# A graph-attention layer: head-key bursts in pairs over two sets of PSUM pairs, row flags through DRAM, 64-output matmuls first in the attention sum

## The chip, the cores and the metric

The kernel runs on one core of one Trainium2 chip, in one launch. The time is device microseconds of one execution of the whole program; the figure given for a kernel is the median over its runs. A profile is one more execution, recorded by the hardware profiler. The engines are PE (TensorE, the matrix unit, which loads 128-row weights and streams columns of up to 512 against them), DVE (VectorE), ACT (ScalarE), POOL (GpSimd) and SP (which here only starts transfers). PE writes to PSUM, eight banks of 128 partitions by 512 floats; the other engines read the results there and "evacuate" them to SBUF, the on-chip memory that everything else lives in. DMA queues move data between SBUF and DRAM. Each engine works off its own queue in order; between engines there are semaphores only, set by the framework wherever one instruction reads what another has written or reuses a buffer that another has read.

## The reference, cut to what matters

A graph-attention layer over x (16 x 512 x 512, float32), with 16 heads of 32, and only the first 20 nodes of each batch as neighbours, in two directions d (the mask and its transpose):

```python
row_zero = v.sum(-1) == 0
q_exp = where(row_zero[..., None], 0.0, q[:, None, :])
self_feat = concat([v, q_exp], -1) @ W_self.T + b_self
output = self_feat
for d in range(2):
    A = (adj if d == 0 else adj.swapaxes(1, 2))[:, :, :20, :]
    cond, vb = A.sum(-1), A @ w_bias + b_bias
    kv = self_feat[:, :20]
    qh = heads(self_feat @ Wq[d].T + bq[d]);  kh = heads(kv @ Wk[d].T + bk[d])
    aff = where(cond > 0, qh . kh / sqrt(32), NEG) + vb
    output += heads_out(softmax(aff) @ kv, Wout[d]) + bout[d]
result = v + relu(output)
```

Three things of it matter here. The term of q enters a row only where the row's sum isn't zero, so each batch needs 512 *row flags*, 0 or 1, on all 128 partitions. The scores need no q projection per row: Wq is multiplied into the keys once, which gives 512 "head keys" per head, neighbour and direction, and the scores are then one product of `self_feat` with them. And the output projection is multiplied into the neighbours' features once (the "values").

## The kernel before, in words

**Stages.** The kernel has a setup, and then a loop over the 16 batches. The setup loads the weights, makes the neighbours' features `kvT` (512 x 320: 16 batches of 20), and from them all keys, values and biases; the loop makes `self_feat` of a batch, its scores in four tiles of 128 rows, the softmax and the weighted sum of the values (`attend`). The first products of batch 0 are made at the end of the setup.

**Bursts of head keys.** `key_rows` (the kind "r" below; PSUM tile `ps_k`, L588) makes 128 rows of the keys per call, as differences to neighbour 0, so 19 columns per batch; there are 8 calls, 2 directions by 4 groups of four heads. A unit of head-key work is one group of 128 output features, one group of four heads, one direction and one batch. There are 512 units, taken 25 or 26 at a time: 20 *bursts*, each of one to three *runs* of consecutive batches (mostly two). In `keys(runs)` a run is four matmuls (L676), one for each head of its group, on 32 rows and 128 outputs, with 19 columns per batch, up to 304. The four heads go to the four banks of two pairs of PSUM banks; a pair is one tile of the pool `ps_s`, which has two of them, so one burst fills the pool and the next has to wait until both are read. For each run ACT (L691) evacuates the first pair, for two heads, and DVE (L693) the second. Both write the tile `st`; when a group's last run is there, POOL copies batch 0's part to `g0` (L697) and SP stores the rest to `g1_d` and `g_d` in DRAM.

**Blocks between the bursts.** Between two bursts PE gets a *block* of other work, during which ACT and DVE empty the pairs. The blocks use single banks of the pool `ps_acc`, of which there are four, by `bank(name)`. Their kinds are

- "m", `bias_terms` (DVE alone), "b", `biases`: DVE adds `bq` to `bqw` (L610), ACT makes four pieces of `bqbd` (L612), POOL adds two small ones;
- "c", `bias_scores`: four small matmuls into `ps_c` (L624), then ACT's copy into the stage `c` (L629), POOL's addition (L633) and four small DMAs on POOL's queue to `cq_d` (L635), which `load_cq` later reads back;
- "v" and "w", `values`: one step is eight matmuls of 512 columns into `ps_v` (L649), and four steps make a result, which DVE copies (L655) and POOL's queue stores to `vw_d` (L659);
- "n", `row_flags` of batch 0 or 1: one matmul of 512 columns with a 128x128 matrix of ones (`ps_nz`, L213), which sums the row sums over the partitions onto all 128 of them, and DVE's test into `nzs[b]`;
- "p", `block_product`: one of the seven products of batch 0 (banks of 256 columns, L283), then a step of `partial` or `joined` on DVE.

The first matmul of `row_flags(b)` needs `row_sums(b)`: three additions on POOL (L207, L209) into a tile `rx` of the tag "xn". That tag has two buffers; `rx0`, the stage `c` and `rx1` take turns in them.

**Order.** Nothing is planned by the framework; everything is in the order in which it is written (`manual_schedule`), per engine. The loop over the bursts writes, after each burst, its block by a list of kinds, and after that the work of other engines for batch 0, by the burst's number: `mask_mul`, `mask_count`, `mask_sum` and `mask_spread` (POOL's product with the label weights, L314; DVE's count and POOL's test, L323; DVE's sum, L328; ACT's copies), `clear_first` (POOL's queue, zeros to `bd_d`, L148), `row_sums(1)`, `blocks(0)` (only makes a list of copies in DRAM), `load_cq(0)`, `new_self(0)` and `x_sum`, six `spill`s (each a copy of that list on POOL's queue) and `full_add`.

**attend.** Each batch's values are laid out so that the sum over 40 neighbours is done in pieces of 32 rows: four pieces with 32 outputs and then two with 64, each on four row groups, all added in the same four banks (L435). The first kind starts the addition, the second ends it.

The old order of blocks, one word for each burst from the fifth to the last, and the list of `attend`:

```python
plan = "mmvv bvv vvc vvc vvn vvw vvw vw wn p p p p p p p".split()
for first, runs in ((True, ((0, 1, 0), (3, 1, 2), (4, 1, 2), (7, 1, 4))), (False, ((1, 2, 1), (5, 2, 3)))):
```

Of the kernel before, what the change touches and what calls it, by code (L numbers as in the profile page):

```python
# [18 lines left out]
def gat_kernel(  # L19
# [20 lines left out]
    nc = tc.nc  # L40
    B, F, N = xT.shape
# [23 lines left out]

    def bank(name, at=None):

        tag = {} if at is None else {"bufs": 1}
        return acc["pool"].tile([P, 512], F32, tag="acc" if at is None else f"acc{at}", name=name, **tag)

    ctx.enter_context(tc.manual_schedule())

# [111 lines left out]
    def spill(n, queue=nc.sync):  # L184

        for _ in range(n):
            queue.dma_start(*copies.pop(0))
# [21 lines left out]
            nc.gpsimd.tensor_add(t, t, xs[b][:, k])  # L209

    def row_flags(b):
        ps = bank(f"ps_nz{b}")
        nc.tensor.matmul(ps[:, :N], ones, rss[b], start=True, stop=True)  # L213
        nzs[b] = load.tile([P, N], F32, tag="nz", name=f"nz{b}")
        nc.vector.tensor_scalar(nzs[b], ps[:, :N], 0.0, None, ALU.not_equal)


    def weight_sums():
# [100 lines left out]
    def mask_count(b, h):  # L319
        a = adjs[b, h]  # L320
        cond = msk.tile([P, 2 * S], F32, tag="cond", name=f"cond{b}_{h}")
        nc.vector.tensor_reduce(cond, a.rearrange("p t (m l) -> p (t m) l", l=L), AX.X, ALU.add)
        nc.gpsimd.tensor_scalar(prods[b, h][:, :, L], cond, 0.0, NEG, ALU.is_le, ALU.mult)  # L323
# [102 lines left out]
    def attend(b, banks, tiles=slice(0, NT), start=True, stop=True):  # L426


        wt = wts[b][:, tiles].rearrange("p t (g w) -> p (t g) w", g=HL)
        vd = vds[b].rearrange("p e i g -> p (e i g)")  # L430
        for first, runs in ((True, ((0, 1, 0), (3, 1, 2), (4, 1, 2), (7, 1, 4))), (False, ((1, 2, 1), (5, 2, 3)))):
            for at, n, j in runs:
                for a in range(HL):
                    r = bass.ts(a, R)
                    nc.tensor.matmul(  # L435
                        banks[a][bass.ds(at // 2 * DH, n * DH)].rearrange("p (t n) -> p t n", n=32),
                        vd[r, bass.ds(at * DH, n * DH)], wt[r, :, bass.ts(j, 32)],
                        start=start and first, stop=stop and not first,
                    )
# [15 lines left out]
        outs.clear()  # L455


    with tc.tile_pool(name="setup", bufs=1) as sp, tc.tile_pool(name="ps_acc", bufs=4, space=PSUM) as acc["pool"]:
        wq_sb = sp.tile([P, 2, C, F], F32, name="wq_sb")
        wo_sb = sp.tile([P, 2, C, F], F32, name="wo_sb")  # L460
        khD = sp.tile([P, 2 * C, B * ND], F32, name="khD")
# [15 lines left out]
        with tc.tile_pool(name="setup_k", bufs=1) as sk:  # L477
# [11 lines left out]
            for k in range(C):  # L489
# [1 line left out]
                    out=sel, in_=sel, pattern=[[-1, B]], compare_op=ALU.not_equal, fill=1.0,  # L491
                    base=-k * DH, channel_multiplier=1,
                )
            warm = bank("ps_warm")
            for _ in range(7):
                nc.tensor.matmul(warm[:, :P], ones, ones, start=True, stop=True)

# [85 lines left out]
            def key_rows(d, jc):  # L583

                ps = bank(f"ps_k{d}{jc}")
                for k in range(C):
                    for a in range(HL):
                        nc.tensor.matmul(  # L588
                            ps[bass.ts(a, R), :BM], wk_sb[d][:, k, bass.ds(jc * P + a * R, R)], kvT[:, k],
                            start=(k == 0), stop=(k == C - 1),  # L590
                        )
# [26 lines left out]
        with tc.tile_pool(name="setup_g", bufs=4) as sg:  # L618
# [82 lines left out]
            def block_product(n):  # L701
# [7 lines left out]
                f(*args)  # L709


            steps = {
                "b": [(biases, ())],
                "c": [(bias_scores, (d,)) for d in range(2)],
                "m": [(bias_terms, (d, c)) for c in range(C) for d in range(2)],
                "n": [(row_flags, (b,)) for b in range(2)],
                "p": [(block_product, (n,)) for n in (1, 2, 6, 7, 5, 4, 3)],
                "v": [(values, (t, (d,), k)) for t in range(2) for d in range(2) for k in range(C)],
                "w": [(values, (2, (0, 1), k)) for k in range(C)],
            }  # L720
# [13 lines left out]
            rest = [(d, hg) for hg in range(C) for d in range(2)]  # L734
            first = None
            for n, runs in enumerate(bursts):
                for i in range(len(rest)):
                    if i < (4 if n == 0 else 1) or any(fc == 0 and (d, hg) == rest[0] for fc, hg, d, _, _ in runs):
                        key_rows(*rest.pop(0))
                if n == 4:  # L740
                    values(*steps["v"].pop(0)[1])
                keys(runs)
                if rest:
                    for kind in "mm" if n else ():
                        f, args = steps[kind].pop(0)
                        f(*args)
                    continue
                first = n if first is None else first
                for kind in plan[n - first] if n - first < len(plan) else ():
                    f, args = steps[kind].pop(0)  # L750
                    f(*args)
                if n == 7:
                    mask_mul(0, 0)
                if n == 8:
                    mask_count(0, 0)
                if n == 10:
                    mask_sum(0, 0)
                    load_cq(0)
                if n == 7:
                    clear_first()  # L760
                if n == 9:
                    row_sums(1)
                    copies = blocks(0)
                if n > 13:
                    spill(1, nc.gpsimd)
                if n == 11:
                    new_self(0)
                    for i in range(1, 5):
                        x_sum(0, i)
                if 10 < n < 15:  # L770
                    mask_spread(0, 0, (n - 11,))
                if n == 14:
                    mask_mul(0, 1)
                if n == 15:
                    mask_count(0, 1)
                if n == 17:
                    full_add(0, 0)
# [308 lines left out]
```

## Time and profile before

| | us |
|---|---|
| median of 3 runs | 582.9 (582.06 to 583.93) |
| the profiled execution's own time | 582.57 |
| its span in the profile | 580.7 |
| PE busy | 574.0 (99%) |
| DVE, POOL, ACT busy | 489.8, 404.2, 395.8 |
| mean granted clock of PE | 0.999 |
| first burst to first block product | 26.10 to 72.30 |
| first block product to the loop | 72.30 to 91.33 |
| the loop and the end | 91.33 to 580.70 |

All times within the execution are microseconds from the start of the span. A row of the chain of work that ended last gives the start, the length, the engine and the group of instructions. A row of the groups of instructions gives the busy time, the engine, the line, the operation, out<-in with shapes, the count and, in brackets, the idle time of that engine just before and what ended it. PEld is PE's loading of weights, which overlaps the matmuls. "Busy" for PE is from the first to the last of a sequence of pipelined matmuls, with their ends modelled.

### The profile page before, as it was taken

The page shows a single profiled execution, that of the slowest core. Times are in us where ns is not written, and L with a number is a line of the kernel's source. Part 1 is how long each engine was busy: PE and PEld are TensorE (multiplying, and loading weights), DVE is VectorE, ACT ScalarE, POOL GpSimd, SP SyncE. Part 2 cuts the span into 40 slices and gives each one's busy share as a digit, 9 for nine tenths or more (in the row PEclk, how much of TensorE's full clock was granted, in tenths as well). Part 3 has the DMA queues.
Part 4 walks back from the last instruction along what each step waited for, and adds up shares of the span by engine and source line. Part 5 has one row for each costly group of instructions (what it writes and reads, how often), then busy time and mean ns, then how long its engine had stood idle before and what let it go on. Part 6 is the DMA issues. An engine that isn't in the chain of part 4 may idle for free.

```text
span 580.7 us, 30994 instructions
## 1 busy us (share of the span) xinstructions
PE 574.0 (99%) x13496; PEld 431.6 (74%) x13496; DVE 489.8 (84%) x786; ACT 395.8 (68%) x1170; POOL 404.2 (70%) x383
## 2 busy tenths in 40 slices
PE   8999999999999999999999999999999999999996
PEld 6444458878878787878778787887887878787873
DVE  0475676979898989898999999898989898989896
ACT  1334454587877777778786868687887877777671
POOL 2626976748687776858585867786868677685875
PEclk9999999999999999999999999999999999999999
DMA  8998997857675767777576767566657666674404
GB/s 290 387 399 300 332 362 274 231 144 222 202 239 177 215 200 198 218 181 229 171 215 166 219 166 219 166 205 181 202 162 223 197 191 182 196 205 109 148 19 146
DMA packets 98787, 123.26 MB, mean 212 GB/s; under 512 B 18876, under 2 KB 66968, under 8 KB 96604
## 3 DMA queue, kind: packets, MB, share of 16 engines
q1 hardware_dynamic: 96124, 117.80, 65.5%
q0 software_dynamic: 1392, 2.43, 1.8%
q8 instruction: 106, 1.74, 1.2%
q10 hardware_dynamic: 1136, 1.06, 0.5%
q14 instruction: 29, 0.24, 0.1%
HBM read 82.30 MB, written 40.24 MB: 211 GB/s over the span
## 4 chain that ended last, share of the span: by engine, by line
PE 94%; DVE 3%; DMA 1%; issue 0%; POOL 0%; SPq 0%; ACT 0%; DVEq 0%; POOLq 0%; ACTq 0%
PE ps_s L365 45%; PE ps_a L283 19%; PE ps_c L283 9%; PE ps_o L435 5%; PE ps_d L283 5%; PE ps_v L649 3%; PE ps_k L588 3%; DMA ws_q<-in_wsT 1%; PE ps_kv L537 1%; DVE o L444 0%; PE ps_nz L213 0%; DVE o L1023 0%; DVE wt L424 0%; DVE ps_s L383 0%; DVE sm L415 0%
## 5 line engine op out<-in xcount | busy, mean ns | idle before, releaser
L365 PEld LDWEIGHTS ps_s<-g,sf 128*32 128x32 f32 x8192 | 263.0, 110 | 21.5 <-issue 13.9
L365 PE MATMUL ps_s<-g,sf 128*32 128x152 f32 x8192 | 278.1, 293 | 0.3 <-issue 0.2
L337 ACT COPY both<-add 32x80 f32<-32x80 f32 x512 | 130.9, 256 | 60.3 <-DVE add L328 54.4
L417 POOL TENSOR_TENSOR s<-s,sm 128x640 f32<-128x640 f32 x63 | 80.2, 1274 | 95.5 <-DVE sm L416 73.4
L344 POOL TENSOR_TENSOR full<-cq,both 128x640 f32<-128x640 f32 x64 | 100.3, 1567 | 27.1 <-issue 21.2
L317 ACT ACTIVATE prod<-adj,wb_sb 128x80 f32<-128x80 int32 x330 | 112.4, 432 | 0.0
L392 ACT ACTIVATE s<-s 128x640 f32<-128x640 f32 x63 | 46.5, 738 | 56.5 <-DVE s L387 56.1
L449 POOL TENSOR_TENSOR o<-o,x 128x512 f32<-128x512 f32 x60 | 76.6, 1299 | 0.0
L379 DVE TENSOR_TENSOR full<-ps_s,full 128x608 f32<-128x608 f32 x63 | 48.7, 773 | 22.5 <-PE ps_s L365 19.2
L283 PE MATMUL ps_a<-t,ws_s 128*32 128x246 f32 x1024 | 60.0, 371 | 0.0
L415 DVE TENSOR_REDUCE sm<-s 128x32 f32<-128x640 f32 x63 | 50.8, 807 | 10.6 <-ACT s L392 10.4
L383 DVE TENSOR_REDUCE ps_s<-full 128x32 f32<-128x640 f32 x63 | 52.2, 828 | 2.2
L424 DVE STREAM_TRANSPOSE wt<-s 128x640 f32<-128x640 f32 x63 | 52.8, 838 | 0.6 <-POOL s L417 0.6
L387 DVE TENSOR_TENSOR s<-full,ps_s 128x640 f32<-128x640 f32 x63 | 51.5, 818 | 1.1
L289 DVE SCALAR_TENSOR_TENSOR sf<-nz,qw,ps_a 128x246 f32<-128x246 f32 x128 | 51.6, 443 | 0.3
L283 PEld LDWEIGHTS ps_a<-t,ws_s 128*32 128x32 f32 x1024 | 33.9, 110 | 17.5 <-issue 0.9
L328 DVE TENSOR_REDUCE add<-prod 128x80 f32<-128x960 f32 x32 | 36.8, 1149 | 6.8 <-ACT prod L317 4.0
L446 ACT ACTIVATE o<-o,bo 128x512 f32<-128x512 f32 x60 | 38.2, 709 | 0.6 <-DVE o L444 0.6
L248 POOL TENSOR_TENSOR t<-x 128x492 f32<-128x492 f32 x32 | 36.7, 1148 | 1.6 <-DMA g_d<-st 1.5
L248 POOL TENSOR_TENSOR t<-x,t 128x492 f32<-128x492 f32 x32 | 36.7, 1148 | 1.3
L435 PE MATMUL ps_o<-wt,vd 32*32 32x512 f32 (+5 forms) x816 | 37.6, 578 | 0.0
L444 DVE TENSOR_TENSOR o<-ps_o,sf 128x512 f32<-128x512 f32 x60 | 36.7, 668 | 0.0
(225 smaller groups left out, 712.6 us busy)
## 6 DMA issues: line engine op xcount, KB each, us to landing
g<-g_d SPq DMA_DIRECT2D x60, 304.0 KB
g_d<-st SPq DMA_DIRECT2D x16, 1064.0 KB
out_T<-o SPq DMA_DIRECT2D x60, 256.0 KB
xn<-in_xn SPq DMA_DIRECT2D x56, 256.0 KB
x<-in_xT SPq DMA_DIRECT2D x56, 256.0 KB
adj<-in_adj SPq DMA_DIRECT2D x60, 220.0 KB
nz<-nz_d SPq DMA_DIRECT2D x14, 256.0 KB
wk<-in_wkT SPq DMA_DIRECT2D x2, 1024.0 KB
```

What stands on the lines that cost most here:

```text
L248: done["xsum"] = nc.gpsimd.tensor_sub(t, one, two)
L283: nc.tensor.matmul(to, lhs, x[:, k], start=start, stop=stop, skip_group_check=n != 2)
L289: done["partial"] = nc.vector.scalar_tensor_tensor(to[:, i], nzs[b][:, half(l)], qw[:, 2 * f + i, b : b + 1], parts[b, "a"][i][:, :HN], AL ...
L317: nc.scalar.activation(p[:, :, l], a[:, :, l], AF.Identity, scale=wb_sb[:, l : l + 1])
L337: done["spread"] = nc.scalar.copy(adds[b, h][bass.ts(a, R), :, g], add[r].rearrange("p (t m) -> p t m", t=2))
L344: done["full"] = nc.gpsimd.tensor_add(f, cqs[b].unsqueeze(1).to_broadcast(shape), adds[b, nt // 2][:, nt % 2].unsqueeze(2).to_broadcast(sh ...
L365: nc.tensor.matmul(to, sfs[b][:, k, bass.ds(nt * P + (2 * g + j) * R, R)], of, start=(onto is None and k == 0 and (whole or j == 0)), stop ...
L383: nc.vector.tensor_reduce(mx, f, AX.X, ALU.max)
L417: done["normal"] = nc.gpsimd.tensor_mul(s, s, sm.unsqueeze(3).to_broadcast(full))
L424: nc.vector.transpose(wts[b][:, nt], s.rearrange("p a h m -> p (a h m)"))
L435: nc.tensor.matmul(banks[a][bass.ds(at // 2 * DH, n * DH)].rearrange("p (t n) -> p t n", n=32), vd[r, bass.ds(at * DH, n * DH)], wt[r, :, ...
L449: nc.gpsimd.tensor_add(o[:, c], o[:, c], xs[b][:, c])
```

## The change

Four things are changed.

1. *Double bursts.* The pool `ps_acc` now holds two pairs in place of four single banks, so there are two sets of two pairs: set 0 is the pool `ps_s`, set 1 is `ps_acc`. In the first seven steps two bursts follow each other directly, the first into set n and the second into set 1 - n, and n changes from step to step. The block behind them takes its banks, two by two, from the pairs of set n (`fill_from(n)`), which the first burst had filled and ACT and DVE have to empty first; the first pair it gets is ACT's. Seven steps with doubles, then six with one burst and one product each, make the same 20 bursts.
2. *The order* of all work of the bursts' part, which was spread over a list of kinds, `if n == ...` lines and the way in which `key_rows` were taken, is one string of kinds; new letters stand for the work of the other engines: R `row_sums(1)`, M, C, S, T the four mask steps, L `load_cq(0)`, N `load_nz`, D `blocks(0)` and `clear_first`, F `new_self`, X `x_sum`, Z a spill, A `full_add`. "b" stands at the end of step 2, behind four value steps, in place of ahead of two; "R" behind the first half of the values of step 3; the two row flags in steps 2 and 5.
3. *Row flags.* Four matmuls of 128 columns, each with 32 columns of ones, put the sums of the four quarters of a batch's rows on the four groups of 32 partitions of one bank. DVE tests 128 columns, SP stores four rows to `nz_d`, and `load_nz` (which the loop has used for the later batches) reads them back to all partitions.
4. *attend* does the two pieces with 64 outputs first and then the four with 32, in all batches.

The loop's order is otherwise as it was.

```diff
     def bank(name, at=None):
 
-        tag = {} if at is None else {"bufs": 1}
-        return acc["pool"].tile([P, 512], F32, tag="acc" if at is None else f"acc{at}", name=name, **tag)
+        if at is None:
+            if not acc["left"]:
+                t = pair(acc["from"], name)
+                acc["left"] = [t[:, 0], t[:, 1]]
+            return acc["left"].pop(0)
+        return acc["pool"].tile([P, 512], F32, tag=f"acc{at}", name=name, bufs=1)
+
+    def pair(n, name):
+
+        return (acc["pool"] if n else ps_s).tile([P, 2, 512], F32, tag="s", name=name)
+
+    def fill_from(n):
+
+        acc["from"], acc["left"] = n, []
...
     def row_flags(b):
+
         ps = bank(f"ps_nz{b}")
-        nc.tensor.matmul(ps[:, :N], ones, rss[b], start=True, stop=True)
-        nzs[b] = load.tile([P, N], F32, tag="nz", name=f"nz{b}")
-        nc.vector.tensor_scalar(nzs[b], ps[:, :N], 0.0, None, ALU.not_equal)
+        for a in range(HL):
+            nc.tensor.matmul(ps[bass.ts(a, R), :P], ones[:, :R], rss[b][:, bass.ts(a, P)], start=True, stop=True)
+        t = msk.tile([P, P], F32, tag="nzf", name=f"nzf{b}", bufs=1)
+        nc.vector.tensor_scalar(t, ps[:, :P], 0.0, None, ALU.not_equal)
+        nc.sync.dma_start(nz_d[b].rearrange("(a n) -> a n", a=HL), t[0:P:R])
...
-        for first, runs in ((True, ((0, 1, 0), (3, 1, 2), (4, 1, 2), (7, 1, 4))), (False, ((1, 2, 1), (5, 2, 3)))):
+        for first, runs in ((True, ((1, 2, 1), (5, 2, 3))), (False, ((0, 1, 0), (3, 1, 2), (4, 1, 2), (7, 1, 4)))):
...
-    with tc.tile_pool(name="setup", bufs=1) as sp, tc.tile_pool(name="ps_acc", bufs=4, space=PSUM) as acc["pool"]:
+    with tc.tile_pool(name="setup", bufs=1) as sp, tc.tile_pool(name="ps_acc", bufs=2, space=PSUM) as acc["pool"]:
...
-            warm = bank("ps_warm")
+            fill_from(1)
+            warm = pair(1, "ps_warm")[:, 0]
...
-            def keys(runs):
-
-
-                pairs = [ps_s.tile([P, 2, 512], F32, tag="s", name=f"ps_g{runs[0]}{i}") for i in range(2)]
+            def keys(runs, n):
+
+
+                pairs = [pair(n, f"ps_g{runs[0]}{i}") for i in range(2)]
...
-            plan = "mmvv bvv vvc vvc vvn vvw vvw vw wn p p p p p p p".split()
...
+            def later():
+
+                copies.extend(blocks(0))
+                clear_first()
+
+            steps = {
+                "r": [(key_rows, (d, hg)) for hg in range(C) for d in range(2)],
...
+                "n": [(row_flags, (b,)) for b in range(2)],
...
+                "R": [(row_sums, (1,))],
...
+                "D": [(later, ())],
...
+            do("rrrr")
+            n = 0
+            for kinds in "+mrmmrmmr +mrnmmvvvvb +ccvvvvRM +vvvvDCN +nvvvvSL +wwwwFXXXXT +pTZ pTMZ pTCZ pZ pAZ pZ pN".split():
+                keys(bursts.pop(0), n)
+                if kinds[0] == "+":
+                    keys(bursts.pop(0), 1 - n)
+                    fill_from(n)
+                    n = 1 - n
+                do(kinds.strip("+"))
```

More of the change, by code (lines that the diff above doesn't have):

```diff
@@ L709, in block_product @@
                 f(*args)
[L712 to L720, printed above, removed]
-            plan = "mmvv bvv vvc vvc vvn vvw vvw vw wn p p p p p p p".split()
             units = [(fc, hg, d, b) for fc in range(C) for hg in range(C) for d in range(2) for b in range(B)]
@@ L733, in gat_kernel @@
                 bursts.append(runs)
[L734 to L749, printed above, removed]
+            copies = []
@@ new lines, in later @@
+            def later():
[3 more added lines that the diff above has]
+                "r": [(key_rows, (d, hg)) for hg in range(C) for d in range(2)],
+                "b": [(biases, ())],
+                "c": [(bias_scores, (d,)) for d in range(2)],
+                "m": [(bias_terms, (d, c)) for c in range(C) for d in range(2)],
+                "n": [(row_flags, (b,)) for b in range(2)],
+                "p": [(block_product, (n,)) for n in (1, 2, 6, 7, 5, 4, 3)],
+                "v": [(values, (t, (d,), k)) for t in range(2) for d in range(2) for k in range(C)],
+                "w": [(values, (2, (0, 1), k)) for k in range(C)],
+                "R": [(row_sums, (1,))],
+                "M": [(mask_mul, (0, h)) for h in range(2)],
+                "C": [(mask_count, (0, h)) for h in range(2)],
+                "S": [(mask_sum, (0, 0))],
+                "T": [(mask_spread, (0, 0, (i,))) for i in range(4)],
+                "L": [(load_cq, (0,))],
+                "N": [(load_nz, (b,)) for b in range(2)],
+                "D": [(later, ())],
+                "F": [(new_self, (0,))],
+                "X": [(x_sum, (0, i)) for i in range(1, 5)],
+                "Z": [(lambda: spill(1, nc.gpsimd), ())] * 6,
+                "A": [(full_add, (0, 0))],
+            }
@@ L750, in gat_kernel, with do @@
+            def do(kinds):
+                for kind in kinds:
                     f, args = steps[kind].pop(0)
                     f(*args)
[L752 to L777, printed above, removed]
+            do("rrrr")
```

## The prediction

> **What bounds the kernel now.** I read the page first (busy times, the chain that ended last), then the work of each engine in stretches of time, then the chain and the timelines of the setup.
>
> ```profile
> span 580.7 us, 30994 instructions
> ...
> PE 574.0 (99%) x13496; PEld 431.6 (74%) x13496; DVE 489.8 (84%) x786; ACT 395.8 (68%) x1170; POOL 404.2 (70%) x383
> ...
> PE 94%; DVE 3%; DMA 1%; issue 0%; POOL 0%; SPq 0%; ACT 0%; DVEq 0%; POOLq 0%; ACTq 0%
> ```
> ```profile
> 26.10:72.30 46.20, 46.18 (x584) 20.18 (x588) 30.55 (x62) 20.08 (x52) 29.65 (x40) 1.00 0.95 347
> 72.30:91.33 19.03, 19.03 (x345) 11.33 (x348) 14.32 (x28) 10.46 (x26) 12.90 (x19) 1.00 1.00 363
> 91.33:580.70 489.37, 484.40 (x12389) 385.27 (x12380) 439.20 (x683) 360.39 (x1083) 350.33 (x305) 1.00 0.64 187
> ```
>
> The columns of the second view are the stretch, its length, busy PE, PEld, DVE, ACT and POOL, the granted clock (1.00 throughout), DMA share and GB/s. PE is the bound in every stretch: what the change is worth is what PE's queue gains or loses. The change works in the first stretch, from the first burst (26.10) to the first block product (72.30); from there to the loop (91.33) one burst and one product alternate as before. In the first stretch PE is never idle, but "busy" holds the turns between shapes of matmul. The chain shows them:
>
> ```profile
> 36.19 0.23 PE _g(0, 2, 0, 14, 16)0_449 L676 x2
> ...
> 37.66 2.29 PE ps_k L588 x32
> ...
> 56.51 1.06 PE ps_nz L213 x2
> ...
> 58.58 2.71 PE ps_v L649 x24
> 61.29 0.46 PE s_g(2, 0, 0, 0, 16)0_732 L676 x2
> ...
> 61.76 0.24 PE s_g(2, 0, 0, 0, 16)0_732 L676 x2
> ...
> 62.02 0.15 PE s_g(2, 0, 0, 0, 16)0_732 L676 x2
> ...
> 62.18 0.15 PE s_g(2, 0, 0, 0, 16)0_732 L676 x2
> ...
> 62.34 2.71 PE ps_v L649 x24
> 65.05 0.30 PE _g(2, 0, 1, 10, 16)0_767 L676 x2
> ...
> 66.17 1.85 PE ps_v L649 x16
> ```
>
> A burst of two runs is four pieces and lasts 1.05 (61.29 to 62.34), one of three runs 1.12 (65.05 to 66.17); the fourth burst took 1.47 (36.19 to 37.66), 0.3 of it a wait for its key rows. The first piece takes 0.46, its twin with the same 304 columns 0.24: entering a burst costs 0.22. Sixteen value matmuls take 1.85, twenty-four 2.71: 0.86 per step of eight, and 0.13 fixed for each block between bursts. The row flags take 1.06.
>
> **The change, part by part.** I count from the start of the first burst to the first block product; the setup after it and the loop keep their order.
>
> 1. Flags. Four matmuls of 128 columns, each into another 32 output partitions, stand for one of 512. A step of eight (two passes of four such tiles, 512 columns) takes 0.86, so a quarter of the columns takes 0.21, with a little entry 0.24. Twice 1.06 - 0.24: **-1.6**. The result now goes through DRAM. No row prices that trip; the nearest are the small transfers of POOL's queue (5.9 from issue to landing, row below). The first flags are issued in step 2, read in step 4 and used after step 7, more than 25 us later, the second ones only in the loop: nothing, even at three times that price. Two loads of 256 KB are more work for a DMA share of 0.95, some 1.5 us at 347 GB/s, with no PE instruction behind them until then. DVE's test shrinks from 512 to 128 columns; off the path.
>
> 2. Whole blocks. Thirteen blocks lie between the first fourteen bursts, six remain: 7 x 0.13, **-0.9**.
>
> 3. Double bursts. Were nothing waited for, the second burst of each pair would save its entry: 7 x 0.22 = -1.5. But the block behind a double takes its banks from the set of the first burst, and the first pair it gets is the one that ACT empties.
>
> ```profile
> 41.75 1.92 PE L649 MATMUL ps_v<-wo_sb,kvT 128*32 128x512 f32 x16
> 41.86 1.04 ACT L691 ACTIVATE st<-s_g(0, 3, 0, 7, 16)0_502 128x342 f32<-128x342 f32 x2 [1.56 <-PE s_g(0, 3, 0, 7, 16)1_503 L676]
> 62.59 1.25 DVE L693 TENSOR_SCALAR st<-s_g(2, 0, 0, 0, 16)1_733 128x608 f32<-128x608 f32 x2 [1.60 <-issue]
> 47.74 1.13 ACT L691 ACTIVATE st<-_g(1, 0, 1, 10, 16)0_566 128x228 f32<-128x228 f32 x3 [0.61 <-PE _g(1, 0, 1, 10, 16)1_567 L676]
> 46.04 0.16 DVE L610 TENSOR_TENSOR bqw<-bqw,bq_sb 128x8 f32<-128x8 f32 x1
> 46.12 0.68 DVE L655 COPY v<-ps_v 128x512 f32<-128x512 f32 x1
> 46.23 0.89 ACT L612 ACTIVATE bqbd<-bqw 32x8 f32<-32x8 f32 x4 [0.28 <-DVE bqw L610]
> 50.13 0.41 ACT L629 COPY c<-ps_c 128x304 f32<-128x304 f32 x1 [1.27 <-PE ps_c L624]
> ```
>
> ACT begins 0.11 after PE has turned away from a burst (41.75, 41.86) and needs 1.04 to 1.13, taken as 1.07 for two runs; a hand-over between engines takes 0.03 (46.04 + 0.16 to 46.23), I count 0.05. So a double lasts 1.05 + 0.11 + 1.07 + 0.05 = 2.28 where PE's work alone would end at 1.05 + 0.83 = 1.88: PE waits 0.40, more than the entry it saves. As two single bursts it took 2.10, or 2.17 where one has three runs. By the lists of bursts the second has three runs four times (2.28 against 2.17: +0.11), the first twice (1.12 + 0.11 + 1.13 + 0.05 = 2.41: +0.24), neither once (+0.18): 1.1, less the 0.3 that the fourth burst no longer waits: **+0.8**. Bounds: -1.5 without the wait; +2.2 if the block waits for DVE's half (1.25) instead.
>
> The Trainium skill, TensorEngine Tiling, PSUM Bottleneck, speaks against this part: tiling speeds up TensorE but not the evacuation of PSUM, which may become the bottleneck. By that rule part 3 is the +0.8 that I take; by PE's rows alone it would be -1.5, and the whole sum -2.4. ACT's rows above side with the rule.
>
> 4. The biases ("b") now stand behind four value steps, at the end of step 2. DVE copies the values after PE's last matmul there (0.68), adds (0.16), ACT then makes `bqbd` (0.89): done 1.75 after step 3 starts, while ACT is wanted for the fifth burst 1.12 after the start. PE waits for that evacuation: **+0.6**.
>
> 5. The row sums of batch 1 (POOL) are now emitted behind the two bias scores, and PE meets the flags at the head of the block of step 5.
>
> ```profile
> 50.63 0.71 POOL L633 TENSOR_TENSOR c<-c,bb_sb 128x320 f32<-128x320 f32 x1 [1.52 <-ACT c L629]
> 51.64 2.52 POOL L635 DMA_DIRECT2D cq_d<-c  x4 [0.30 <-POOL c L633]
> 54.40 1.47 POOL L659 DMA_DIRECT2D vw_d<-v  x2
> 59.44 2.12 POOL L314 TENSOR_TENSOR prod<-prod,wb_sb 128x880 f32<-128x880 f32 x1
> 61.49 0.96 POOL L148 DMA_DIRECT2D bd_d<-zero  x1
> 62.44 0.32 POOL L697 COPY g<-st 128x152 f32<-128x152 f32 x1
> 62.86 0.59 POOL L323 TENSOR_SCALAR prod<-cond 128x80 f32<-128x80 f32 x1
> 63.75 1.14 DVE L328 TENSOR_REDUCE add<-prod 128x80 f32<-128x960 f32 x1
> 64.63 1.28 POOL L207 TENSOR_TENSOR rx<-x 128x512 f32<-128x512 f32 x1
> 65.99 2.63 POOL L209 TENSOR_TENSOR rx<-rx,x 128x512 f32<-128x512 f32 x2
> cq_d<-c POOLq DMA_DIRECT2D x8, 5.0 KB, 5.9
> ```
>
> POOL: two bias scores of 0.71 + 0.30 + 2.52 = 3.53, a value's DMAs 1.47, the sums 3.99 (64.63 to 68.62): 12.5. It can begin when ACT has copied the first score: 1.75 + 1.04 + 1.07 + 0.41 + 0.05 = 4.3 after the start of step 3; the sums are ready at 16.8. PE: step 3 takes 2.84 to its block, then two scores of 0.51 (304 of 512 columns of a step of 0.86), four value steps and 0.13, 4.6: step 4 starts at 7.4; a double of 2.41 and 3.57 of values later, step 5 at 13.4; its double has a first burst of three runs too, so PE wants the sums at 15.8. It waits **+1.0** (between 0 and 2, as the POOL chain is 1 us shorter or longer).
>
> 6. What DVE waits for next: the mask sum in step 5 stands behind POOL's product (2.12), two copies (0.32), a value's DMA (half of 1.47), `clear_first` (0.96) and a test (0.59), to 21.9 after the start of step 3. DVE is there at 21.4 and takes 1.14, so the two evacuations behind it (1.25 each) end at 25.6; step 7 needs their pair at 26.5. Nothing, with 0.9 in hand; a POOL chain longer by more than that stops PE here too.
>
> 7. The key stores on SP keep their order and queue; the six spills of POOL move by at most one burst. Nothing. SP's flag stores wait for DVE's test, with only later stores behind them.
>
> 8. Wide matmuls first in `attend`, 15 times in the loop and twice at the end.
>
> ```profile
> 160.21 0.25 PEld L435 LDWEIGHTS ps_o<-wt,vd 32*32 32x32 f32 x32 [0.24 <-issue]
> 161.29 0.27 PEld L435 LDWEIGHTS ps_o<-wt,vd 32*64 32x64 f32 x16 [0.84 <-issue]
> 162.38 0.16 PEld L365 LDWEIGHTS ps_s<-g,sf 128*32 128x32 f32 x8 [0.81 <-issue]
> ```
>
> The narrow phase takes 1.08, the wide one 1.09, with three turns of shape in either order. The new neighbours (128-row to 64-wide, 64-wide to 32-wide, 32-wide to 128-row) are in no row. I take **0**; a turn costs 0.13 to 0.22 above, so half of one either way bounds it at 0.1 each, 1.7 in all.
>
> Sum: -1.6 - 0.9 + 0.8 + 0.6 + 1.0 = **-0.1 us**. The profiled execution took 582.57 (580.7 of span, 1.9 around it), 0.3 under the median of 582.9; on the median the forecast is 582.8. Differences under 0.3% (1.75 us) I call no change: a measurement of this kernel can hardly tell them.
>
> **The rivals.**
>
> *Faster: PE's gain comes through.* If the block behind a double needn't wait for ACT (another pair first, or half a pair), parts 1 to 3 are -4.0, and if then POOL keeps up, that is all: 578.9. With parts 4 and 5 in full it is -2.4: 580.5. For it: PE really has these turns to lose. Against: a pair is one tile, and ACT reads both its banks to the last of its instructions. It decides where the waits of parts 3 to 5 together stay under 2.2 of the 3.9 that I count (1.5 + 0.8, 0.6, 1.0). Middle 580.3.
>
> *Slower: the row sums wait for a landing.* `rx1` takes a buffer of two that `rx0` and the stage `c` had. I take that of `rx0`, free early. If it is that of `c`, the sums can't start until the last bias score's DMA, issued at about 10.7 after the start of step 3, has landed 5.9 later, at 16.6: ready at 20.6 in place of 16.8, and PE's first flag matmul waits 3.8 longer: 586.6. For it: in the old order the sums (64.63) began behind other work of POOL, so the trace doesn't tell which buffer they got. Against: `rx0` is the one that came free first. It decides once a landing is more than 4 us behind its issue.
>
> *The widths matter.* 17 times 0.1 either way: 581.1 or 584.5, inside no change unless something adds to it.
>
> **How the numbers follow.** No change, as forecast: 0.60, within 581.1 to 584.5. Faster: 0.22, nearly all from the first rival. Slower: 0.18: 0.12 for the landing, 0.06 for POOL's or DVE's lateness in parts 5 and 6 going beyond what I have in hand, or the widths. The range goes down to the faster rival's middle, a little below (580.0), and up into the slower one's lower half (585.6); each end leaves about 1 in 10 outside.
>
> **What would show it.** Right: seven stalls of PE of 0.3 to 0.5 before the blocks behind the doubles, put down to ACT's evacuation; one near 1 before the flags of step 5, put down to POOL's sums; the loop's length 489.4 as before; attend phases of 1.08 and 1.09. Wrong: blocks that start within 0.15 of the second burst's end (faster rival); flags that wait 3 us or more, with the sums begun at a DMA's landing (slower rival); a loop longer or shorter by more than 1 us (widths, or a late load at its start).

## The result, and the profile after

The changed kernel took 591.84 us (median of 4 runs, 591.17 to 592.30) against 583.05 for the kernel before: 1.0146 times as long, 95% interval 1.0127 to 1.0166. The forecast was no change, 580.0 to 585.6. The profiled execution took 591.72, with a span of 589.9 against 580.7.

The page of the changed kernel, busy times and the chain by engine:

```profile
span 589.9 us, 31016 instructions
...
PE 573.1 (97%) x13508; PEld 434.7 (74%) x13508; DVE 488.0 (83%) x786; ACT 394.8 (67%) x1170; POOL 403.2 (68%) x383
...
PE 93%; issue 2%; ACT 1%; DMA 1%; DVE 1%; SPq 0%; DVEq 0%; ACTq 0%
```

PE is 0.9 us less busy than before (574.0), and the span is 9.2 longer: PE waits. Where, the work by stretches tells (first burst at 28.78, first product at 80.59, loop at 99.98; columns as in the prediction's second view):

```profile
28.78:80.59 51.81, 45.29 (x592) 22.07 (x592) 29.14 (x62) 18.46 (x50) 25.79 (x38) 0.97 0.80 289
80.59:99.98 19.39, 19.39 (x340) 11.69 (x344) 14.43 (x29) 11.33 (x30) 14.88 (x21) 1.00 1.00 361
99.98:589.90 489.92, 483.08 (x12392) 386.01 (x12384) 438.85 (x683) 360.24 (x1083) 349.62 (x305) 1.00 0.66 188
```

The first burst starts 2.7 us later than before (28.78, 26.10), the stretch to the first product takes 5.6 more (51.81, 46.20), the rest of the setup 0.4 more, the loop 0.5 more. PE's groups in the setup of the changed kernel, those that waited, with the wait and what ended it in brackets:

```profile
20.94 4.51 PE L604 MATMUL ps_k<-kvT,wk 128*32 128x320 f32 x64 [0.96 <-DVE khD L611]
26.42 2.36 PE L604 MATMUL ps_k<-kvT,wk 128*32 128x320 f32 x32 [0.96 <-DVE khD L611]
31.11 2.36 PE L604 MATMUL ps_k<-kvT,wk 128*32 128x320 f32 x32 [0.18 <-ACT st L707]
34.49 4.51 PE L604 MATMUL ps_k<-kvT,wk 128*32 128x320 f32 x64 [1.02 <-DVE khD L611]
44.69 0.43 PE L227 MATMUL ps_k<-rx,ones 128*32 128x128 f32 x8 [1.12 <-DVE khD L611]
51.40 0.72 PE L640 MATMUL ps_c<-khD,bqbd 128*32 128x304 f32 x8 [0.94 <-ACT st L707]
52.66 0.72 PE L640 MATMUL ps_c<-khD,bqbd 128*32 128x304 f32 x8 [0.54 <-ACT c L645]
...
65.24 0.43 PE L227 MATMUL ps_nz<-rx,ones 128*32 128x128 f32 x8 [0.47 <-POOL rx L221]
67.08 5.34 PE L665 MATMUL ps_nz<-wo_sb,kvT 128*32 128x512 f32 x32 [1.41 <-DVE nzf L229]
...
74.74 3.64 PE L665 MATMUL ps_v<-wo_sb,kvT 128*32 128x512 f32 x32 [0.33 <-ACT st L707]
```

In the kernel before, PE has no such wait in the setup; its first four key rows are one unbroken group:

```profile
17.15 8.95 PE L588 MATMUL ps_k<-kvT,wk 128*32 128x320 f32 x128
```

Six of the changed kernel's waits are of one kind, and the prediction has none of it. Key rows wait for `khD`, which DVE makes from the key rows before them; the flags at 44.69 do the same; the second bias scores wait for ACT's copy of the first; the values at 67.08 wait for DVE's test of the flags. Nothing that they read depends on what they wait for. What they have in common with it is the pair: each writes the second bank of a tile whose first bank is being read. The row at 67.08 even carries the name of the flags (`ps_nz`), because the two banks are one tile. The six add up to 0.96 + 0.96 + 1.02 + 1.12 + 0.54 + 1.41 = 6.0 us, 1.92 of them ahead of the first burst.

### The profile page after: what moved, and what is told of

The parts are those of the page before. It is cut to its first block, busy times and chain, and to the rows that moved or that the text cites. A ratio compares the mean times of both kernels' runs of the same rounds, so it can differ in the third digit from the quotient of the medians.

```text
span 589.9 us, 31016 instructions
## 1 busy us (share of the span) xinstructions
PE 573.1 (97%) x13508; PEld 434.7 (74%) x13508; DVE 488.0 (83%) x786; ACT 394.8 (67%) x1170; POOL 403.2 (68%) x383
## 3 DMA queue, kind: packets, MB, share of 16 engines
q8 instruction: 106, 1.74, 1.3%
## 4 chain that ended last, share of the span: by engine, by line
PE 93%; issue 2%; ACT 1%; DMA 1%; DVE 1%; SPq 0%; DVEq 0%; ACTq 0%
PE ps_s L380 45%; PE ps_a L298 18%; PE ps_c L298 8%; PE ps_o L450 6%; PE ps_d L298 5%; PE ps_k L604 3%; PE ps_v L665 2%; DMA ws_q<-in_wsT 1%; ACT st L707 1%; PE ps_o L796 1%; PE ps_kv L553 1%; DVE khD L611 0%; PE ps_s L369 0%; ACT kh L610 0%; PE g(3, 2, 0, 14, 16)0_1058 L692 0%
```

## The experiments

All ratios are to the kernel before, on the same chip and in the same rounds; 0.1% is 0.58 us.

**e1_mixed: the second banks.** Up to the first product a block's banks alternate between the set's two pairs:

```diff
-            if not acc["left"]:
-                t = pair(acc["from"], name)
-                acc["left"] = [t[:, 0], t[:, 1]]
-            return acc["left"].pop(0)
+            if acc["mixed"]:
+                i = len(acc["left"])
+                acc["left"].append(pair(acc["from"], name) if i < 2 else acc["left"][i - 2])
+                t = acc["left"][i][:, i // 2]
+                if i == 3:
+                    acc["left"] = []
+                return t
```

> The changed kernel, but the blocks take their banks alternately from the two pairs of the set (first bank of ACT's pair, first of DVE's, then the second ones), up to the first block product. Theory (a pair is one tile, so a matmul into its second bank waits until the first bank has been read): the six waits of 0.96, 0.96, 1.02, 1.12, 0.54 and 1.41 us before second banks go, some 6.0, and with the last of them the stretch at half clock behind it, some 1.9: 591.8 - 7.9 = 583.9, between 582.5 and 585.5. Rival (the double bursts themselves outrun ACT and DVE): the waits move to the next evacuation, and at least 589 remains.

587.88 us, ratio 1.0072 (1.0060 to 1.0084): it takes back half of the loss. In its trace, PE's waiting groups of the same part:

```profile
29.01 6.67 PE L612 MATMUL ps_k<-kvT,wk 128*32 128x320 f32 x96 [0.18 <-ACT st L715]
41.27 3.64 PE L673 MATMUL ps_k<-wo_sb,kvT 128*32 128x512 f32 x32 [0.81 <-DVE khD L619]
47.77 1.23 PE L648 MATMUL ps_c<-khD,bqbd 128*32 128x304 f32 x16 [0.94 <-ACT st L715]
55.01 3.64 PE L673 MATMUL ps_v<-wo_sb,kvT 128*32 128x512 f32 x32 [0.33 <-ACT st L715]
61.63 0.43 PE L234 MATMUL ps_nz<-rx,ones 128*32 128x128 f32 x8 [1.00 <-POOL rx L228]
```

Three calls of key rows now run through (x96), both bias scores too (x16), the values behind the second flags don't wait. One wait of the kind is left (0.81), where three banks follow each other quickly and the third is again the first's neighbour. So the cause of the six waits is shown. But 7.9 us were expected from it and some 4 came (1.46% to 0.72%). 1.9 of the 7.9 stood for a stretch at half clock that the last section describes, and that shows no cost. The first burst is 2.1 earlier and the loop 6.0; the loop itself became 2.5 longer. What PE's chain has at the loop's start, in the kernel before, the changed one and e1_mixed:

```profile
95.19 0.24 issue
107.81 1.60 issue
101.76 2.70 issue
```

In these pieces PE stands still and waits for nothing but its own instructions.

**e4_halves: the pairs without the double bursts.** This was to be the kernel before with its four single banks as two pairs, and nothing else. It has no time: in the old order of work the engines then wait for each other in a circle. So what the pairs cost without the doubles and the new order was not measured.

**e2_attend: the order of the attention sum alone.** Before, with only the two lists of `attend` exchanged.

> The kernel before with the wide matmuls of attend first and nothing else. Prediction's part 8: 0, so 583.0, and the whole phase 2.17 us long in both. Rival (a turn of shape costs 0.1 more or less): 581.3 or 584.7, phases of 2.07 or 2.27.

583.86 us, ratio 0.9999 (0.9988 to 1.0009). PE's weight loads of one such phase, the next tile's scores behind it:

```profile
162.02 0.23 PEld L435 LDWEIGHTS ps_o<-wt,vd 32*64 32x64 f32 x16 [0.24 <-issue]
163.06 0.29 PEld L435 LDWEIGHTS ps_o<-wt,vd 32*32 32x32 f32 x32 [0.81 <-issue]
164.19 1.84 PEld L365 LDWEIGHTS ps_s<-g,sf 128*32 128x32 f32 x60 [0.84 <-issue]
```

164.19 - 162.02 = 2.17, as in the rows of before (162.38 - 160.21). The order is worth nothing that these runs can tell (some 0.6 us either way). The trace has two stalls "for issue" in the loop, 0.86 at 96.7 and 0.97 at 116.8, where that of the kernel before has 0.24, though the two kernels take the same time. So the size of such stalls differs between executions, and one profile gives it only roughly.

**e3_flags: the row flags alone.** Before, with the new `row_flags`, `load_nz(0)` behind the eleventh burst's work and `load_nz(1)` behind the last burst's.

> The kernel before with the row flags by four matmuls of 32 outputs and through DRAM, and nothing else. Prediction's part 1: -1.6, so 581.4; its two blocks with flags shorter by 0.8 each. Rival (the shorter flags leave less cover for the evacuation behind them, or the two loads hold up others): between 582.4 and 583.6.

585.24 us, ratio 1.0034 (1.0023 to 1.0046): slower. Its setup did gain: from first burst to first product 44.9 against 46.2, so 1.3 where 1.6 were forecast. It lost more at the beginning of the loop:

```profile
94.34 4.33 PE L368 MATMUL ps_s<-g,sf 128*32 128x152 f32 x127 [0.59 <-issue]
101.18 4.08 PE L368 MATMUL ps_s<-g,sf 128*32 128x152 f32 x120 [2.50 <-issue]
```

Again PE waits for its instructions, 3.1 us in all. The DMA view has a queue for them, by its size: 106 packets of 16 KB in a run of the kernel before, 1.74 MB, which are some 64 bytes for each of PE's 13,496 matmuls and 13,496 weight loads, or one packet for 256 of them. The queues (packets, MB, share of the 16 engines' time) in the same stage, in the kernel before (93.5 to 101.2, no long stall) and in e3_flags (92.5 to 98.8, the 6.3 us up to the long stall):

```profile
q1 hardware_dynamic: 310, 1.19, 41.7%
q0 software_dynamic: 256, 0.25, 17.0%
q8 instruction: 2, 0.03, 1.6%
```
```profile
q1 hardware_dynamic: 497, 2.06, 95.5%
q0 software_dynamic: 72, 0.08, 4.1%
```

With the 16 DMA engines full of stores and loads (95.5%) no block of PE's code came for 6.3 us. The scores at 94.34 above use one up (127 matmuls and as many loads) in 4.33.

**e9_loads: the bytes alone.** Before, with two loads of 256 KB that nobody uses, at the two places of e3_flags:

```diff
+                    nc.sync.dma_start(extra, xT[2, :P])
+                if n == 19:
+                    nc.sync.dma_start(extra, xT[3, :P])
```

> The kernel before with two loads of 256 KB that nothing uses, on SP's queue where e3_flags has its loads of the flags (after the eleventh burst's work and at the end of the setup). PE's order is that of before. Theory (the setup's DMA work ends later by these bytes, and PE's code blocks of 16 KB wait behind it): 0.5 MB at 347 GB/s are 1.5 us; the stalls around the loop's start grow from 0.24 to between 1.5 and 3: 584.5 to 586. Rival (the loss of e3_flags came from its matmuls, test or store): 583.2 within 0.6.

585.09 us, ratio 1.0032 (1.0021 to 1.0044), the same loss as e3_flags with none of its matmuls, and clear of the 583.2 of the rival. PE's chain has stalls again:

```profile
96.22 1.15 issue
...
101.71 1.13 issue
```

Half a megabyte more through the DMA engines in the setup costs 1.9 us, though no instruction of PE waits for it. That the 1.9 us are these stalls is the likeliest reading, but e2_attend's trace has 1.8 us of them without a loss. e3_flags lost 2.0 after a gain of 1.3, so 3.3 in all: the bytes explain 1.9 of it. The other 1.4 may be the gain itself, a PE that is earlier than its code; no run separates that.

**e12_flags_late.** As e3_flags, with `load_nz(1)` moved into the loop, behind the first scores.

> As e3_flags (before, with only the new row flags), but batch 1's flags are loaded in the loop, behind the first scores. Its setup keeps the 1.3 us that e3_flags gained from the first burst to the loop; 256 KB less at the end of the setup. Theory: the stalls of 0.59 and 2.50 shrink by 0.75 to 1.5 us: 585.2 - 1.1 = 584.1, between 583.5 and 584.7. Rival (not the load, but a PE that is earlier by 1.3 us than its code): the stalls stay, 585.2.

584.08 us, ratio 1.0013 (1.0002 to 1.0025): 1.2 us back for 256 KB less. The stalls for code are 2.1 us in its trace, 3.1 in that of e3_flags. The flags gain 1.3 in PE's queue and still don't pay.

**e5_late_nz, e6_order, e7_oneflag, e8_singles: mending the change.** e5_late_nz is e1_mixed with `load_nz(1)` in the loop. e6_order is that, and

```diff
-"+mrmmrmmr +mrnmmvvvvb +ccvvvvRM +vvvvDCN ..."
+"+mrmmrmmr +mnrmmbRvvvv +ccvvvvM +vvvvDCN ..."
```

> As e1_mixed, but the load of batch 1's flags (256 KB) is issued in the loop, behind the first scores, and not at the end of the setup. In e1_mixed PE stood still for 0.19, 0.41, 2.70 and 1.02 us shortly before and after the loop's start, with nothing that it waited for but its own instructions (before: 0.24). Theory (PE's code blocks of 16 KB come through the same 16 DMA engines and stand behind the setup's stores and loads): these stalls shrink by 0.75 (256 KB at 347 GB/s) to 2 us: 586.3, between 585.7 and 587.2. Rival (the stalls have nothing to do with that load): 587.9 within 0.6.

> As e5_late_nz, and the order mended at three places: in step 2 the flags ahead of the key rows and the biases ahead of the values, the row sums of batch 1 right behind them in step 2 in place of step 3. PE's waits of 0.81 (values behind key rows), 0.94 (bias scores behind bqbd) and 1.00 (flags behind the sums) of e1_mixed go. Theory (PE's queue alone sets the time): 2.7 less than e5_late_nz, 583.6. Rival (the setup's DMA work ends no earlier, so PE's code comes no earlier either): the setup is 2.7 shorter, but the stalls at the loop's start grow by 1 to 2.7: 584.6 to 586.3.

e5_late_nz took 587.38 (1.0065, 1.0052 to 1.0078), not to be told from e1_mixed and above the 585.7 to 587.2 that its theory gave; the longest stall of its trace is 1.30. e6_order took 587.16 (1.0059, 1.0047 to 1.0072), 3.6 more than PE's queue alone promised. Of its three waits the mended order removed less than the sum says: from the first burst to the first product it takes 46.2 us, 0.9 less than e1_mixed and as long as before, since new waits of 0.39 and 0.27 for the evacuations stand where the row sums were late, and the delay of the biases only moved. Two lines of DVE and one of POOL in that stage of e6_order:

```profile
42.11 1.76 DVE L628 SCALAR_TENSOR_TENSOR bqt<-wq_sb,br_sb 128x512 f32<-128x512 f32 x1
43.91 1.11 DVE L634 TENSOR_TENSOR bqw<-bqw,bq_sb 128x8 f32<-128x8 f32 x1
41.59 3.40 POOL L228 TENSOR_TENSOR rx<-rx,x 128x512 f32<-128x512 f32 x2
```

In e1_mixed the same two DVE instructions take 0.69 and 0.16, and in the changed kernel POOL's two additions take 2.61. Beside each other, where the mended order puts them, they are all slower. ACT gets `bqw` for `bqbd` at 45.06 only, and from the end of the values to the bias scores PE takes 3.0 us, against 2.9 in e1_mixed: part of its wait now lies inside the double burst. That DVE and POOL hold each other up is the likeliest reading (e7_oneflag's trace has 1.16 and 1.75 for two such DVE instructions in the same place), but no run separates the two.

Behind the first product e6_order loses more than it gained: 1.78 for code, 0.62 ahead of a burst, for ACT, which itself was held up, 0.55 for a sum of POOL's and 0.84 for DVE's transpose ahead of the first weighted sum. ACT's and DVE's waits between 70 and 98 us for the landing of a store, whose `st` tile they are to write again (us in all, times, the longest):

```profile
ACT st L715 <- DMA g_d<-st: 1.8, 2, 1.4
DVE st L717 <- DMA g_d<-st: 1.0, 1, 1.0
```

The kernel before has no such wait there, e1_mixed has 1.7 and 1.6, e12_flags_late 0.8 and 0.7. So late stores reach PE by two ways, its code and the `st` tiles. The expectations of e5_late_nz (for e1_mixed) and e10_half_order (for e6_order) put all four stalls of each down to code; only the longest is.

e7_oneflag is e6_order with the old flags. e8_singles is e6_order with every burst single, into the first pool's pairs, and the blocks in the second pool's, by the string `mr mmrmmr mnr mmbRvv vv ccvv vvM vv vvDCN nvv vvSL ww wwFXXXXT pTZ pTMZ ...`.

> As e6_order, but with the old row flags (one matmul of 512 columns, DVE's test on 512, no DRAM, no load). PE's queue alone: the setup 1.6 longer, so 1.6 more than e6_order. Rival (half a megabyte less through the DMA engines pays it back): within 0.6 of e6_order, with shorter stalls at the loop's start.

> As e6_order, but every burst is single, into the pairs of the first pool, with a block behind each but with the same work in the same order; the blocks take the second pool's pairs alternately. Prediction's parts 2 and 3 say that seven doubles gain 0.9 by fewer blocks and lose 0.8 by the waits: 0 against e6_order, within 0.8. PE's turns alone (7 x 0.13 and 7 x 0.22) would make it 2.4 slower in the setup.

e7_oneflag: 586.25 (1.0043, 1.0030 to 1.0056); e8_singles: 585.89 (1.0036, 1.0022 to 1.0050). Each undoes a part that saves PE time (0.7 us in the first stretch for the flags, 0.3 for the doubles) and each came out faster by its median, by 0.9 and 1.3 us, with intervals that overlap with e6_order's.

**e10_half_order, e11_half_before, e14_half_after: the stores halved.** To take the DMA load away, only batches 2 to 8 of each group's keys are stored, in e11_half_before (the kernel before), e14_half_after (the changed one) and e10_half_order (e6_order); the later batches load earlier ones' keys. By the profile, 8.7 MB of 40.2 MB written go (e10_half_order's expectation has 7.4):

```diff
-        src = g1_d if b == 1 else g_d[:, :, b - 2]
+        src = g1_d if b == 1 else g_d[:, :, (b - 2) % 7]
-                        nc.sync.dma_start(g_d[C * fc + hg], st[:, 2:])
+                        nc.sync.dma_start(g_d[C * fc + hg], st[:, 2:9])
```

> The kernel before with the same half stores (output of batches 9 to 15 not the reference's). It has only 0.24 of such stalls: 583.0 within 0.6 by the DMA theory, which says that the order before just keeps the DMA engines fed early enough. The difference of e10_half_order to this run is what the mended change is worth to PE alone: 0 within 1 by the prediction's sum of -0.1. If the old stores cost PE time elsewhere too, this run is clearly faster.

> The changed kernel with the half stores of e10_half_order and e11_half_before (output of batches 9 to 15 not the reference's). If PE's own waits in the setup are the whole loss of the change (first burst 2.7 later, 5.7 more to the first product, 0.4 to the loop), they all remain and only the stall of 1.60 in the loop goes: 590, within 1. If the DMA engines, which stood idle for some 8 us of the setup in the changed kernel, carry the loss, most of it goes: 582 to 585.

> As e6_order, but only half of each group's keys is stored to g_d (batches 2 to 8 of 2 to 15), and the later batches load the keys of earlier ones, so the output of batches 9 to 15 is not the reference's; the loop's loads are the same. 7.4 MB less to store in the setup. Theory (DMA backlog holds up PE's code): the stalls of 0.62, 1.78, 0.55 and 0.84 us around the loop's start go, 587.2 - 3.8 = 583.4, within 1. Rival (these stalls have another cause): 587.2 within 0.6.

| | all stores | half the stores |
|---|---|---|
| before | 1 | 0.9969 (0.9957 to 0.9980) |
| changed | 1.0146 (1.0127 to 1.0166) | 1.0082 (1.0068 to 1.0096) |
| mended (e6_order) | 1.0059 (1.0047 to 1.0072) | 0.9980 (0.9970 to 0.9990) |

With the DMA engines relieved, the changed kernel is 1.13% behind the kernel before, 6.6 us: that is what PE's own waits cost. The remaining 0.33%, 1.9 us, of the 1.46% go with the stores; the intervals together leave 0.06% to 0.60% for it. Neither reading of e14_half_after's expectation was right alone: it came out between them. For the mended kernel it is the other way round: 0.11% (0.6 us, not clear of 0 by the intervals) behind with half the stores, 0.59% (3.4 us) with all: nearly all of what is left goes with the stores (0.48%, 0.28% to 0.68% by the intervals). The same stretch at the loop's start, first e6_order, then e10_half_order (stretch, length, busy PE and so on, granted clock, DMA share, GB/s):

```profile
96.00:112.00 16.00, 13.66 (x372) 12.22 (x368) 10.41 (x16) 6.68 (x22) 9.40 (x10) 1.00 0.55 168
```
```profile
96.00:112.00 16.00, 16.00 (x444) 14.13 (x440) 14.81 (x24) 8.06 (x23) 12.41 (x12) 1.00 0.71 180
```

2.3 us of standing still are gone there with the stores, 1.78 of them for code and 0.55 for POOL. But just behind that stretch, at 113.6, e10_half_order has one stall of 1.00 for code, with the DMA share at 0.92 from 108 to 112 and no packet of code in these 4 us; so half the stores don't remove every stall. In e14_half_after the 1.60 of the changed kernel are gone. The kernel before itself gains 0.31% by halving the stores, so even it pays a little.

**How the DMA engines are fed.** The changed and the mended kernels differ from the one before in what the DMA engines get to do, e6_order too, whose stretch from first burst to first product is as long. From 36 to 66 us, before and then the changed kernel:

```profile
36.00:66.00 30.00, 29.98 (x366) 12.46 (x362) 18.66 (x38) 11.71 (x28) 18.24 (x28) 1.00 0.92 331
```
```profile
36.00:66.00 30.00, 26.26 (x360) 12.57 (x348) 16.86 (x37) 11.56 (x29) 15.20 (x22) 1.00 0.66 220
```

| | DMA share, 36 to 66 | share lost against before, us | extra bytes in the setup, us at 347 GB/s | sum | measured loss, us |
|---|---|---|---|---|---|
| changed | 0.66 | 7.8 | 1.5 | 9.3 | 8.5 |
| e1_mixed | 0.81 | 3.3 | 1.5 | 4.8 | 4.2 |
| e5_late_nz | 0.83 | 2.7 | 0.8 | 3.5 | 3.8 |
| e6_order | 0.86 | 1.8 | 0.8 | 2.6 | 3.4 |
| e7_oneflag | 0.82 | 3.0 | 0 | 3.0 | 2.5 |
| e8_singles | 0.85 | 2.1 | 0.8 | 2.9 | 2.1 |
| e3_flags | 0.93 | -0.3 | 1.5 | 1.2 | 2.0 |
| e9_loads | 0.91 | 0.3 | 1.5 | 1.8 | 1.9 |
| e12_flags_late | 0.93 | -0.3 | 0.8 | 0.5 | 0.8 |

In each row the time that the DMA engines lost in the middle of the setup, and the bytes added to it, agree with the loss of the kernel within 0.9 us. This is a fit and not an experiment: the stretch was chosen when the losses were known. In the changed kernel the DMA engines idle because PE's waits hold up the bursts, so its 7.8 us and the 6.6 us of PE's waits are largely one delay seen from two sides, and not to be added. From 66 to 96 us the share is 0.97 to 1.00 in all of them, so there is no room in which to make up what is lost earlier. The stores can only start when a group of bursts is done; e6_order has its bursts two by two, with blocks of 3.6 to 6.7 us between, and its share from 36 to 66 is lower than that of before though PE is as fast. That stores in such lumps are the cause is a possible reading of e6_order and e8_singles and is not shown; their difference (1.3 us) is not clear of the intervals. No kernel of this study beats the one before with the reference's output.

## Why the prediction was wrong

*The banks of a block (part 3).* "The block behind a double takes its banks from the set of the first burst, and the first pair it gets is the one that ACT empties": the pair was priced for its first bank only. That a second bank of the same tile waits for the reading of the first was not asked, although the text argues in the first rival that "a pair is one tile". It costs six waits of 0.54 to 1.41 us, and two of them lie ahead of the first burst, in the key rows, which the part left out with "I count from the start of the first burst". This is the step that failed: part 3's +0.8 has no term for them, and they add up to 6.0 us. With the half stores, where little else is left, the change is 6.6 us over the kernel before.

*The loads of the flags (part 1).* "Two loads of 256 KB are more work for a DMA share of 0.95 ... with no PE instruction behind them" was booked as nothing. e9_loads measures it: 1.9 us, most likely by way of PE's own code. The share of 0.95, and of 1.00 behind it, stood in the quoted rows; PE at 99% was taken as the only bound of the setup, when the DMA engines were a second one, just covered.

*What held.* The flags' matmuls gained 1.3 (forecast 1.6). The waits for ACT behind the doubles were 0.18, 0.33, 0.33 and 0.17 where nothing else was late, below the 0.40 forecast: between e8_singles and e6_order parts 2 and 3 together are -0.3 in the first stretch against -0.1, though not cleanly, since e8_singles has a wait of its own there, 1.25 ahead of a burst. The biases' delay showed at the bias scores (0.94, of which 0.33 is the usual wait for ACT: +0.6, as forecast). The row sums came late by 1.00 once the other waits were gone (forecast +1.0; 0.47 in the changed kernel, where PE itself was late). They started right behind a value's DMAs (59.73 + 1.47), with no landing waited for, while the last two bias-score transfers landed at 64.8 and 65.5 by the trace; so the stage's buffer was not the one they got, and that rival fell:

```profile
59.73 1.47 POOL L675 DMA_DIRECT2D vw_d<-v  x2
...
61.21 1.29 POOL L219 TENSOR_TENSOR rx<-x 128x512 f32<-128x512 f32 x1
```

The order in `attend` is worth 0 within 0.6 us, and no wait in PE's list is put down to the mask sum or to a moved transfer (parts 6 and 7). The sum was right for what it looked at: in e14_half_after the stretch takes 50.2 us against 46.2 in e11_half_before, and the four waits for second banks that lie in it make 4.06 there (1.02, 1.12, 0.54, 1.38), which leaves -0.1, as forecast. Part of that is luck: the flags gained less than forecast, and the row sums cost 0.51 there in place of 1.0, because PE was late itself.

*The rule cited in part 3* (the Trainium skill, TensorEngine Tiling, PSUM Bottleneck) pointed the right way: PE does wait for evacuations here, 0.17 to 0.33 us behind a double. It was followed for one bank of each pair only.

## What to carry to other kernels

When PSUM buffers are regrouped, list for every matmul which reads of the same tile come before it, not only of the same bank: two banks in one tile had one release here. Where PE is 99% busy and the DMA share is at 0.95 or more in the same stage, as in this setup, count two bounds, and a gain on one or a few added bytes on the other will show only when both are counted. PE's program is itself a DMA stream here (1.74 MB), so a stall of PE "for issue" behind a stage full of stores is first to be looked for among the bytes.

## What was not expected of the hardware

*PE's code in line with the data.* By the trace's packets the missing block of code began to move at 98.9 in e3_flags, 102.1 in e1_mixed and 107.1 in the changed kernel, and PE went on at 101.2, 104.5 and 109.4: 2.3 to 2.4 us later each time. The two stalls of e9_loads end in the same way, 2.3 us behind packets that began to move at 95.1 and 100.5. The stall (1.6 to 2.7 us at one place) is as large as the largest terms of the prediction's sum.

*Half clock for 3.4 us that shows no cost.* Behind the two waits of 0.47 and 1.41 us the changed kernel's profile shows the granted clock at one half (stretch, length, busy PE, granted clock, DMA share, GB/s):

```profile
67.10:68.00 0.90, 0.90 (x12) 1.00 0.89 326
68.00:69.00 1.00, 1.00 (x12) 0.57 1.09 420
69.00:70.00 1.00, 1.00 (x8) 0.50 1.05 424
```

The 32 value matmuls there take 5.34 against 3.64 with full clock. The Trainium skill, TensorE: Matmul & The Clock Gate, Part 1, says that the clock is halved after at least one idle window of some 3.4 us, that full clock comes back after at least one busy window of that length, and that the windows run freely. The trace agrees on the length of the slow stretch (from 68.1 to 71.5), but it followed less than 2 us of waiting in all, while a stall of 2.70 in e1_mixed, and waits of 0.51 and 1.38 at the same place of e14_half_after, were followed by full clock. What decides it is not shown here. The profiled execution, with a mean clock of 0.995, took 591.72, the three others, with 0.997 and 0.998, 591.17 to 592.30. If their higher clock means that they had no slow stretch (they were not traced), it has no price here. That the stores behind it were the limit anyway fits the table above, but was not tried by itself.
